# A lower least rate of filling, and outputs that begin later in their slot, in the first attention of a two-layer decoder

## The chip, the cores and the metric

The kernel runs on one core of one Trainium2 chip. The metric is the device time of the whole program in microseconds. The time before is 2068.65 us, the median of 3 runs (2068.05 to 2070.13).

## What is computed

The program is a decoder of two layers with a layer norm after each of six parts. Its input x has 8 batches of 256 tokens with 512 features, all in float32. The change touches the first part alone, a differential attention with causal mask, cut here to what matters:

```python
q = (x @ Wq.T).reshape(8, 256, 32, 16)          # 32 query heads of 16
k = (x @ Wk.T).reshape(8, 256, 8, 16)           # repeated 4 times
v = (x @ Wv.T).reshape(8, 256, 4, 32)           # repeated 8 times
scores = where(causal, einsum('bhqd,bhkd->bhqk', q, k) * 16 ** -0.5, min)
attn_out = einsum('bhqk,bhkd->bhqd', softmax(scores), v)
attn = attn_out[:, 0::2] - lambda_full * attn_out[:, 1::2]
attn = attn * rsqrt(mean(attn * attn) + eps) * ln_w * (1 - LAMBDA_INIT)
x = layernorm(x + attn.reshape(8, 256, 512) @ Wo.T)
```

After it follow a long convolution, a mixture of experts, a plain causal attention, a cross attention with a cached context and a routed attention. The second and the last attention use the same planner as the first.

## The kernel before, in words

The tokens are 16 tiles of 128. Four tiles, that is two batches, make a group, so there are four groups (0 to 3). In the first attention a *unit* is one batch and four heads: 8 units for a batch, 16 for a group, 64 in all. The function `causal_attention` (L1316) walks over *slots*, one for each unit, and some more for the tail. In slot u it does, on TensorE in this order:

- the plain scores of unit u (`maxima`, L1370). ScalarE copies them from PSUM (L1387), GpSimd masks them (L1389), and VectorE takes row maxima (L1398). The maxima of a whole batch are split into three bfloat16 terms and turned at the start of the next batch (`turn`, L1415).
- some filling work;
- the numerators of unit u - 10 (`products`, L1471), for which GpSimd has masked and added the weights;
- the weights' scores of unit u - 9 (`weights`, L1430), from which ScalarE makes the exponentials (L1458);
- the denominators of unit u - 10 (`divided`, L1491), with the reciprocal on VectorE (L1503), and then the events of the place "mid";
- filling work again, up to the scores of the next slot.

Plain scores and weights' scores share one PSUM buffer of four banks (`ps_sc`). All other results of TensorE except numerators and denominators go through three PSUM buffers (`pools`, tag "mm").

The *filling* is all other work of TensorE: turning the tiles of x of the next group, its values, keys and queries (four query blocks a batch, of four steps each), and, for each finished batch, its output. The output of a batch comes from `finish` (L510): squares on ScalarE (L580), their sums on TensorE (L532), a turn back (L545), roots on GpSimd (L561), widening on ScalarE (L557), and then for each of the two tiles a scaling (`scaled`, L568; four transposes, then a multiplication on VectorE, L577). `scaled` orders the four output steps of its tile (`out_tile`, L505), each a product of 0.86 by the planner's costs. The last step adds the residual on VectorE and starts the layer norm (`add_norm_later`, L269). In group 3 the sixteen tiles of the context are turned too, one a slot from slot 54 on (`turn_context`, L439). A tile's load into one of two buffers is issued when the tile two places before it has been turned. Tiles 8 to 15 go through one buffer (cT) from which a DMA stores them to DRAM.

The planner decides at build time which filling goes into which slot. Pieces with a due slot stand in `queue`, sorted by it; pieces without stand in `after` with the slot from which they may begin, and those come first. `fill(budget)` takes steps one after the other until at most 0.3 of its budget is left. Costs are the planner's own: 0.86 for a full product and 0.45 for four transposes. The budget of a slot is `rate` (L1610): the larger of a least rate and the sum of what is pressing (`pressure`, L1576: for each due slot, the work up to it divided by the slots that are left) and an eighth of the cost of a batch's output. The first part of it, `short` (L1613 to L1617), is filled between the plain scores and the numerators; the rest goes behind the denominators. `need(u + 1)` (L1563) does at once whatever is due in the next slot, before that slot's scores. `at(slots, place, f)` (L1526) orders an event or, with the place "fill", a piece for `after`. The engines TensorE, VectorE, ScalarE and GpSimd work in the order in which this program writes their instructions; SP issues the DMAs from its own queue.

Of the kernel before, what the change touches and what calls it, by code (L numbers as in the profile page):

```python
# [55 lines left out]
def decoder_kernel(ctx: ExitStack, tc: tile.TileContext, a: dict, out: bass.AP):  # L56
# [212 lines left out]
    def add_norm_later(work, t, ps, at):  # L269

        r = work.tile([P, D], F32, tag="row", name="res", bufs=3)
        nc.vector.tensor_tensor(r, ps, x[t], ALU.add)
        at(1, "mid", norm_later(x[t], r, lambda f: at(0, "end", f)))
# [22 lines left out]
    def diff_attention(xh, ch):  # L296
# [203 lines left out]
        def squares(n):  # L500

            n = n % 2 * KB * S
            return w[:, n : n + KB * S].rearrange("p (k s) -> p k s", k=KB)

        def out_tile(work, pools, t, yT, at):  # L505


            return out_block(pools, yT, t % 2, wo, lambda ps: add_norm_later(work, t, ps, at))

        def finish(work, pools, t0, yT, at):  # L510

            cost = 2 * (0.4 + TR + KB * MM)
            if t0 == NT - 2:
                return cost


            apart = 1 if t0 == NT - 4 else 2
            hurry = t0 == NT - 4
            wide = {}
            sq = squares(t0 // 2)  # L520

            quads = work.tile([P, 32], F32, tag="quads", name="quads", bufs=1)
            nc.vector.tensor_copy(
                quads.rearrange("p (r t) -> p r t", r=8), quad.unsqueeze(1).broadcast_to([P, 8, 4])
            )
            means = work.tile([P, S], F32, tag="means", name="means", bufs=1)

            def sums():

                ps = pools.tile([P, S], F32, tag="mm", name="ps_ss")  # L530
                for k in range(KB):
                    nc.tensor.matmul(  # L532
                        ps[32 * k : 32 * k + 32, :],
                        lhsT=quads,
                        rhs=sq[:, k, :],
                        start=True,
                        stop=True,
                    )
                nc.vector.tensor_scalar(means, ps, 1.0 / 32, EPS, ALU.mult, ALU.add)
                at(0 if hurry else 1, "end" if hurry else "mid", norms)  # L540

            def norms():
                pt = pools.tile([P, 2, P], F32, tag="mm", name="pt_ss")
                for i in range(2):
                    nc.tensor.transpose(pt[:, i, :], means[:, i * P : (i + 1) * P], ident)  # L545
                rr = work.tile([P, 2, H0], F32, tag="rrs", name="rr")
                nc.vector.tensor_copy(
                    rr.rearrange("p i (k t) -> p i k t", k=KB),
                    pt.rearrange("p i (k r t) -> p i k r t", k=KB, t=4)[:, :, :, 0],
                )  # L550
                roots(0, rr[:, 0, :])
                at(apart, "end", lambda: roots(1, rr[:, 1, :]))

            def roots(i, rr):
                def widen():
                    wide[i] = work.tile([P, H0, 32], F32, tag="wide", name="wide")
                    nc.scalar.copy(wide[i], rr.unsqueeze(2).broadcast_to([P, H0, 32]))  # L557

                def root(half):
                    r = rr[:, 8 * half : 8 * half + 8]  # L560
                    nc.gpsimd.tensor_tensor(r, r, neg_half[:, :8], ALU.pow)  # L561

                root(0)
                at(apart - 1, "end", lambda: root(1)) if apart > 1 else root(1)
                at(apart, "end", widen)
                at(apart + 1, "fill", [(TR, lambda: scaled(i))])

            def scaled(i):  # L568
                pt = pools.tile([P, KB, P], F32, tag="mm", name="pt_rr")
                for k in range(KB):  # L570
                    nc.tensor.transpose(
                        pt[:, k, :],
                        wide[i][:, 4 * k : 4 * k + 4, :].rearrange("p t d -> p (t d)"),
                        ident,
                    )
                y = yT[:, :, i * P : (i + 1) * P]
                nc.vector.tensor_tensor(y, y, pt, ALU.mult)  # L577
                at(1, "fill", out_tile(work, pools, t0 + i, yT, at))

            at(1, "start" if hurry else "end", lambda: nc.scalar.activation(sq, yT, AF.Square))  # L580
            at(1 if hurry else 2, "fill", [(0.7, sums)])
            return cost
# [733 lines left out]
    def causal_attention(name, prepare, finish, upb=KB, gather=None):  # L1316
# [18 lines left out]
        with ExitStack() as st:  # L1335
            work = st.enter_context(
                tc.tile_pool(name=f"{name}_work", bufs=2, **({"reuse_waits": "tile"} if name == "r" else {}))
            )
            ps_sc = st.enter_context(tc.tile_pool(name=f"{name}_sc", bufs=1, space=PSUM, reuse_waits="tile"))
            ps_pv = st.enter_context(tc.tile_pool(name=f"{name}_pv", bufs=1, space=PSUM, reuse_waits="tile"))  # L1340
            pools = st.enter_context(tc.tile_pool(name=f"{name}_ps", bufs=3, space=PSUM, reuse_waits="tile"))
# [23 lines left out]
            groups, negT, pT, yT = {}, {}, {}, {}  # L1365
# [160 lines left out]
            def at(slots, place, f):  # L1526


                if place == "due mid":
                    at(slots, "mid", lambda: insort(queue, f, key=lambda piece: piece[0]))  # L1530
                elif place == "fill":
                    after.append((now[0] + slots, f))
                    after.sort(key=lambda piece: piece[0])
                else:
                    events.setdefault((now[0] + slots, place), []).append(f)

            def happen(place):
                for f in events.pop((now[0], place), []):
                    f()
# [18 lines left out]
            def begin(g):  # L1558
                pieces, *groups[g] = prepare(work, pools, g, at, now[0])
                queue.extend((upg * g + slot, steps) for slot, steps in pieces)  # L1560
                queue.sort(key=lambda piece: piece[0])
# [14 lines left out]
            def pressure(u):  # L1576

                total = most = 0.0
                begun = [(due[0], current)] if current and due[0] < units + 99 else []
                for slot, steps in begun + queue:  # L1580
                    total += sum(c for c, _ in steps)
                    most = max(most, total / max(1, slot - u))
                return most

            def sums(u):
# [10 lines left out]

                return rest

            begin(0)
            need(0)  # L1600
            if name == "r":
# [2 lines left out]
            per_batch = 0.0  # L1604
            left = 0.0
            for u in range(units + lag + 2):
                now[0] = u
                happen("start")

                rate = max(2.4, pressure(u) + per_batch / upb)  # L1610
                if u < units:
                    largest = maxima(u)
                    short = max(0.0, min(0.8, rate - 1.8))  # L1613
                    if rate > 2.7:
                        short += (rate - 2.7) / 2
                    if name == "a":
                        short += MM / 2  # L1617
                    left = fill(left + short)
                    rest = sums(u)
                    if name != "a":  # L1620
                        rest()
                        happen("mid")
                    if u >= wait:
                        weights(u - wait)
                    if name == "a":
                        rest()
                        happen("mid")
                    if u % upg == upb and u // upg + 1 < NG:
                        begin(u // upg + 1)
                    left = fill(left + rate - short - MM) - need(u + 1)  # L1630

                    if u and u % upb == 0:
                        turn(u // upb - 1)
                    left = fill(left + MM)
                    largest()
                    if u % upb == upb - 1:
                        split(u // upb)
                else:

                    if u < units + wait:  # L1640
                        weights(u - wait)
                    sums(u)()
                    happen("mid")
                    left = fill(left + rate) - need(u + 1)
                    if u == units:
                        turn(B - 1)
                happen("end")
# [29 lines left out]
    def out_block(pools, yT, i, w, done):  # L1677

        return product_steps(
            lambda: pools.tile([P, D], F32, tag="mm", name="ps_o"),  # L1680
            lambda k: yT[:, k, i * P : (i + 1) * P],
            lambda k: w[:, k, :],
            done,
        )
# [758 lines left out]
```

## Time and profile before

What | Value
--- | ---
median of the runs | 2068.65 us
profiled execution, own time | 2062.48 us
its span, first to last instruction | 2060.7 us
mean granted clock of TensorE | 0.983
score copies of the first attention (L1387) | 64, from 13.88 to 378.87 us
last exponential of the first attention (L1458) | 429.88 us
last output matmuls of the first attention | 451.43 to 453.35 us
first matmuls of the convolution | 460.25 us

Between 140 and 379 us TensorE was busy 219.69 of 239 us, VectorE 189.05, GpSimd 179.11 and ScalarE 136.25. From the 10th copy (slot 9, 48.52 us) to the 64th (slot 63, 378.87 us) a slot took 6.12 us on average; the shortest took 5.22.

How to read it: a row of a timeline has the start in us, the duration, the engine, the line, the operation, what is written and read, the shape, how often, and in brackets how long the engine stood idle before and what ended that. A row of waits has who waited for whom, the sum in us, the number of times and the longest. A matmul in float32 counts as two instructions here, and neighbouring matmuls overlap, so a group's duration is a little longer than its share.

### The profile page before, as it was taken

What the parts mean: (1) busy time and instruction counts of PE and PEld (TensorE: products, weight loads), DVE (VectorE), ACT (ScalarE), POOL (GpSimd) and SP (SyncE); (2) the same over time, 40 slices, a digit from 0 to 9 for tenths busy, and PEclk for the clock granted to TensorE, in tenths of its full rate; (3) what the DMA queues carried; (4) which work ended last, traced back from release to release, by engine and by line L of the source; (5) the groups of instructions that cost most, each with busy time, mean ns of one, the idle gap of its engine ahead of it and who ended that gap; (6) DMA issues with size and microseconds to landing.
All of it is one profiled execution on the core that took longest, in us unless ns stands there. A gap on an engine that the chain in (4) does not pass through costs nothing. (4 is left out here: it accounts for less than half of the span.)

```text
span 2060.7 us, 46451 instructions
## 1 busy us (share of the span) xinstructions
PE 1921.8 (93%) x20142; PEld 1141.9 (55%) x20142; DVE 1253.7 (61%) x1933; ACT 620.1 (30%) x793; POOL 858.0 (42%) x952
## 2 busy tenths in 40 slices
PE   8979999889998998999999999998999999988885
PEld 5545555444443445666555555544888887454443
DVE  4677878758888976122234757456344544437987
ACT  4555555520010003211114434432101011245552
POOL 3687777846556823000014645333100010216763
PEclk9999999989999999999999999999999999999997
DMA  6899953315115125213232212002101000260000
GB/s 230 311 386 380 383 168 84 94 52 212 31 46 184 52 98 188 77 65 129 80 110 84 84 34 83 2 2 81 49 16 41 21 21 1 90 191 15 25 24 32
DMA packets 138044, 219.24 MB, mean 106 GB/s; under 512 B 27440, under 2 KB 52144, under 8 KB 137840
## 3 DMA queue, kind: packets, MB, share of 16 engines
q1 hardware_dynamic: 131376, 195.93, 27.9%
q0 software_dynamic: 6464, 20.32, 2.9%
q8 instruction: 161, 2.64, 0.5%
q14 instruction: 43, 0.35, 0.1%
HBM read 104.42 MB, written 123.34 MB: 111 GB/s over the span
## 5 line engine op out<-in xcount | busy, mean ns | idle before, releaser
L1503 DVE RECIPROCAL rsum<-ps_pv 128x256 f32<-128x256 f32 x128 | 224.5, 1754 | 215.6 <-PE ps_pv L1495 215.4
L182 PE MATMUL ps_y<-kv,wt 128*128 128x512 f32 x640 | 280.0, 596 | 5.2 <-POOL kv L625 2.7
L1398 DVE TENSOR_REDUCE neg<-rows 128x12 f32<-128x1536 f32 x128 | 223.0, 1742 | 53.3 <-POOL rows L1389 53.2
L1458 ACT ACTIVATE pT<-ps_k 128x1536 f32<-128x1536 f32 x128 | 185.7, 1451 | 225.4 <-PE ps_k L1450 218.4
L1459 POOL TENSOR_SCALAR_AFFINE_SELECT pT<-pT 128x1024 f32<-128x1024 f32 x128 | 141.3, 1104 | 217.4 <-ACT pT L1458 217.2
L1387 ACT COPY rows<-ps_q 128x1536 f32<-128x1536 f32 x128 | 184.2, 1439 | 151.0 <-PE ps_q L1378 96.0
L1389 POOL TENSOR_SCALAR_AFFINE_SELECT rows<-rows 128x1024 f32<-128x1024 f32 x128 | 142.3, 1112 | 183.8 <-ACT rows L1387 183.1
L182 PEld LDWEIGHTS ps_y<-kv,wt 128*128 128x128 f32 x640 | 120.8, 191 | 156.3 <-issue 137.7
L1469 POOL TENSOR_TENSOR pT<-pT 128x512 f32<-128x512 f32 x112 | 147.1, 1313 | 9.3
L212 PE MATMUL ps_f<-xT,w_l1a 128*32 128x256 f32 x2048 | 123.4, 385 | 5.5 <-ACT xT L237 4.1
L1164 PE MATMUL po_m<-dn,hT 128*128 (+1 forms) x216 | 100.8, 603 | 4.0 <-issue 2.3
L148 POOL TENSOR_SCALAR rstd<-bn_mv 128x1 f32<-128x1 f32 x80 | 15.8, 198 | 212.5 <-DVE bn_mv L156 206.4
L1143 DVE TENSOR_TENSOR h_b<-h_b,pg 128x352 f32<-128x352 f32 x36 | 18.6, 516 | 124.0 <-ACT h_b L1142 124.0
L1495 PE MATMUL ps_pv<-pT,ones_v 128*32 128x256 f32 (+1 forms) x1152 | 87.1, 381 | 5.2 <-POOL pT L1469 5.1
L212 PEld LDWEIGHTS ps_f<-xT,w_l1a 128*32 128x32 f32 x2048 | 62.9, 111 | 51.2 <-issue 9.0
L663 DVE TENSOR_REDUCE yc<-z 128x64 f32<-128x512 f32 x128 | 86.1, 673 | 5.7 <-issue 5.2
L1279 POOL DMA_INDIRECT y<-ys,slots x4 | 4.0, 1007 | 204.4 <-PE pu L182 203.8
L1378 PEld LDWEIGHTS ps_q<-kT,qT 32*128 32x128 f32 x1536 | 49.5, 188 | 50.5 <-issue 18.1
L182 PE MATMUL pg<-gu,xT_b 128*128 x216 | 72.1, 470 | 3.6 <-ACT xT_b L237 3.6
L1378 PEld LDWEIGHTS ps_q<-kz,qT 32*128 32x128 f32 x1536 | 49.2, 188 | 47.2 <-ACT pT L1458 33.7
L1378 PE MATMUL ps_q<-kz,qT 32*128 32x128 f32 x1536 | 61.5, 289 | 14.3 <-ACT pT L1458 11.6
L1378 PE MATMUL ps_q<-kT,qT 32*128 32x128 f32 x1536 | 61.9, 290 | 12.7 <-ACT pT L1458 8.7
(411 smaller groups left out, 3694.2 us busy)
## 6 DMA issues: line engine op xcount, KB each, us to landing
xs<-zero SPq DMA_DIRECT2D x8, 4352.0 KB
ys<-zero SPq DMA_DIRECT2D x8, 4352.0 KB
filters<-in_L_xattn_k SPq DMA_DIRECT2D x4, 2560.0 KB
first_h<-xs SPq DMA_DIRECT2D x36, 256.0 KB
ys<-y_m SPq DMA_DIRECT2D x36, 256.0 KB
gu<-in_L_ffn_gate_up_proj SPq DMA_DIRECT2D x3, 2816.0 KB
wt<-filters SPq DMA_DIRECT2D x32, 256.0 KB
sorted_x<-zero SPq DMA_DIRECT2D x1, 5120.0 KB
```

The costliest lines, as they stand in the source:

```text
L182: nc.tensor.matmul(ps, lhsT=lhsT(k), rhs=rhs(k), start=(k == 0), stop=(k == n - 1))
L212: nc.tensor.matmul(ps[cs], lhsT=lhsT[:, cs], rhs=rhs, start=start, stop=stop)
L1164: nc.tensor.matmul(po, lhsT=hT[:m, i, :], rhs=dn[i][:m, bass.ds(e, 1), :], start=(i == 0), stop=(i == len(FCH) - 1),)
L1378: nc.tensor.matmul(block[:, s, j, :], lhsT=q(rows, c, b * S + i * P, P), rhs=k(rows, c, b * S + keys * P, P), start=True, stop=True,)
L1387: nc.scalar.copy(d.rearrange("p j s k -> p s j k"), block)
L1389: nc.gpsimd.affine_select(out=rows, in_=rows, compare_op=ALU.is_ge, fill=-FAR, base=0, pattern=[[0, 8], [-1, P]], channel_multiplier=1,)
L1398: return lambda: nc.vector.tensor_reduce(neg[u // upb % 2][:, :, :, c], d, AX.X, ALU.max, negate=True)
L1458: nc.scalar.activation(p[:, 0:3].rearrange("p j s q -> p s j q"), block, AF.Exp)
L1459: nc.gpsimd.affine_select(out=p[:, 0:2].rearrange("p j s q -> p (j s) q"), in_=p[:, 0:2].rearrange("p j s q -> p (j s) q"), compare_op=ALU ...
L1469: nc.gpsimd.tensor_tensor(p[:, 3], p[:, 1], p[:, 2], ALU.add)
L1495: nc.tensor.matmul(ps[32 * s : 32 * s + 32, 1, j * P :], lhsT=ones_v, rhs=p[:, 1, s, :] if j else first[:, :, s, :], start=(j == 0), stop= ...
L1503: nc.vector.reciprocal(r, ps[:, 1, :])
```

## The change

Two things change in the planner's input, and no instruction is added or taken away.

First, the least rate falls from 2.4 to 1.8 for the first attention (its name is "a") and stays at 2.4 for the two others. With a rate of 1.8 the first part of the filling of a slot is 0.43 instead of 1.03.

Second, the four output steps of a tile enter the list of filling only at the place "mid" of the slot after the scaling, that is after the weights' scores and the denominators. Before, they could be the first filling of that slot, in front of numerators and weights' scores.

```diff
@@ -575,7 +575,8 @@
                     )
                 y = yT[:, :, i * P : (i + 1) * P]
                 nc.vector.tensor_tensor(y, y, pt, ALU.mult)
-                at(1, "fill", out_tile(work, pools, t0 + i, yT, at))
+                steps = out_tile(work, pools, t0 + i, yT, at)
+                at(1, "mid", lambda: at(0, "fill", steps))
 
             at(1, "start" if hurry else "end", lambda: nc.scalar.activation(sq, yT, AF.Square))
             at(1 if hurry else 2, "fill", [(0.7, sums)])
@@ -1596,6 +1597,7 @@
 
                 return rest
 
+            least = 1.8 if name == "a" else 2.4
             begin(0)
             need(0)
             if name == "r":
@@ -1607,7 +1609,7 @@
                 now[0] = u
                 happen("start")
 
-                rate = max(2.4, pressure(u) + per_batch / upb)
+                rate = max(least, pressure(u) + per_batch / upb)
                 if u < units:
                     largest = maxima(u)
                     short = max(0.0, min(0.8, rate - 1.8))
```

## The prediction

> **What bounds the kernel now.** First the page. It gives the profiled execution, 2060.7 us of span and 2062.48 us of own time, and shows TensorE as the busiest engine in every slice.
>
> ```profile
> span 2060.7 us, 46451 instructions
> ...
> PE 1921.8 (93%) x20142; PEld 1141.9 (55%) x20142; DVE 1253.7 (61%) x1933; ACT 620.1 (30%) x793; POOL 858.0 (42%) x952
> ```
>
> The change touches only the first attention, so next I read ScalarE's timeline there. Its score copies (L1387) run from 13.88 to 378.87 us, 64 of them, one for each slot; the tail of the stage ends near 457 us.
>
> ```profile
> 109.10 1.45 ACT L1458 ACTIVATE pT<-ps_k 128x1536 f32<-128x1536 f32 x1 [1.26 <-PE ps_k L1450]
> 111.62 1.44 ACT L1387 COPY rows<-ps_q 128x1536 f32<-128x1536 f32 x1 [1.07 <-PE ps_q L1378]
> 114.34 1.45 ACT L1458 ACTIVATE pT<-ps_k 128x1536 f32<-128x1536 f32 x1 [1.28 <-PE ps_k L1450]
> 116.86 1.44 ACT L1387 COPY rows<-ps_q 128x1536 f32<-128x1536 f32 x1 [1.07 <-PE ps_q L1378]
> ```
>
> That is the floor of a slot. There is one buffer for scores, so copy, weights' scores, exponential and next scores take turns: 1.44 + 1.28 + 1.45 + 1.07 = 5.24 us, of which 2.72 from copy to exponential (first half) and 2.52 from exponential to next copy (second half). Slots 18 to 23 have almost no filling and sit at this floor. Eight slots earlier it is another picture:
>
> ```profile
> 69.42 1.45 ACT L1458 ACTIVATE pT<-ps_k 128x1536 f32<-128x1536 f32 x1 [1.28 <-PE ps_k L1450]
> ...
> 72.11 1.44 ACT L1387 COPY rows<-ps_q 128x1536 f32<-128x1536 f32 x1 [0.93 <-PE ps_q L1378]
> ...
> 75.28 1.45 ACT L1458 ACTIVATE pT<-ps_k 128x1536 f32<-128x1536 f32 x1 [1.36 <-PE ps_k L1450]
> ```
>
> Here three query steps of 0.45 us stand in each half. The second half (69.42 to 72.11) took 2.69, 0.17 over; the first (72.11 to 75.28) 3.17, 0.45 over. So a first half hides 0.90 us of filling and a second half 1.18; what is beyond counts in full. Over slots 9 to 62 the excess over 5.24 is 330.35 - 54 x 5.24 = 47.4 us. This is all that the change can win in the body. The chain of waits by engine says what the excess holds besides filling:
>
> ```profile
> PE ps_o L212 <- DVE yT_b L577: 6.5, 4, 1.9
> ...
> PE ps_v L212 <- issue: 2.7, 2, 1.5
> ```
>
> Four output tiles begin in the first half of their slot, before VectorE has scaled their rows (L577), and the weights' scores queue behind them: 6.5 us, in slots 26, 40, 42 and 58. TensorE's timeline shows slot 26, 1.93 us:
>
> ```profile
> 146.05 1.92 PE L212 MATMUL ps_o<-w_l,yT_b 128*32 128x512 f32 x16 [1.93 <-DVE yT_b L577]
> 147.76 0.86 PE L1484 MATMUL ps_pv<-pT,v 128*32 128x256 f32 x16
> ```
>
> In the tail one more wait matters, with a slow TensorE behind it:
>
> ```profile
> 409.64 0.23 PE L1450 MATMUL ps_k<-negT,take 32*128 32x128 bf16 x4
> 412.10 1.51 PE L1484 MATMUL ps_pv<-pT,v 128*32 128x256 f32 x16 [2.23 <-DVE rr L471]
> 413.33 1.55 PE L1495 MATMUL ps_pv<-pT,ones_v 128*32 128x256 f32 x16
> ```
>
> The granted clock from 412 to 416 us was 0.57, and the two groups took 1.51 and 1.55 where others take 0.86 and 0.83.
>
> **The change part by part.** No instruction is added or removed. The planner's choice is arithmetic on the code's own costs (0.86 a product, 0.45 a transpose), so I followed it slot by slot, before and after. The old list agrees with the trace (the two output steps of slot 26, for one). Prices of a step from rows: output, value or key product 0.885 (16 matmuls 1.92, 24 take 2.78), query 0.45, transposed tile 0.55, scaling transposes 0.53, sums 0.45, turned maxima 0.25.
>
> *Head, slots 0 to 8* (no weights yet). Slots 3 to 6 are bound by TensorE: 0.88 of scores and 2.2 to 2.7 of filling, together 13.99 us. At a rate of 1.8 they hold 1.80, 2.25, 2.22 and 1.77, so 4 x 0.88 + 8.04 = 11.6: 2.4 less. Slots 0 to 2 win nothing (slot 2's copy waits for the lambda exponential at 22.53), nor slots 7 and 8, where turning the maxima ends a chain of copy, GpSimd, VectorE and split 6.4 us long. Head: -2.4.
>
> *Body.* The table has the excess over 5.24 in us: measured before; by the rule of 0.90 and 1.18 before; the surplus of measured over rule (waits); the rule on the new lists; what I keep of the surplus and what comes new.
>
> slots | measured | rule | surplus | new rule | new total | change
> 9-17 | 5.5 | 4.5 | 1.0 | 1.9 | 1.9 + 0.6 = 2.5 | -3.0
> 18-24 | 0.8 | 0.8 | 0 | 2.1 | 2.1 | +1.3
> 25-31 | 10.9 | 5.9 | 5.0 | 5.2 | 5.2 + 5.0 - 2.0 + 0.9 = 9.1 | -1.8
> 32-40 | 7.8 | 5.0 | 2.8 | 3.4 | 3.4 + 2.8 - 1.6 = 4.6 | -3.2
> 41-47 | 11.4 | 5.9 | 5.5 | 8.5 | 8.5 + 5.5 - 2.0 = 12.0 | +0.6
> 48-56 | 6.2 | 5.2 | 1.0 | 6.6 | 6.6 + 1.0 - 0.5 + 0.6 = 7.7 | +1.5
> 57-63 | 4.8 | 2.3 | 2.5 | 5.6 | 5.6 + 2.5 - 1.8 + 0.6 + 4.1 = 11.0 | +6.2
>
> Reading it: filling leaves slots 9 to 17 and fills the empty slots 18 to 22. The four waits on L577 go (-2.0, -1.1, -2.0, -1.8, and 0.5 each where sums and an output shared slots 35 and 51): outputs now come after the weights' scores. In slot 26 0.9 comes back, because three transposed tiles stand there in the first half and the third needs the buffer that VectorE is still reading. The price of the lower rate is late work in group 3: the planner's need for slots 41 to 46 rises to a rate of 3.65; in slots 52 and 60 a whole query block is forced in before the next scores (second halves of 3.08 and 3.97 us), and its evacuation (0.38 and the hand-overs, 0.6) then stands between it and the scores: 0.6 each.
>
> The 4.1 in the last row: the context tiles, once one a slot, pile up, and tiles 6, 7 and 8 are turned back to back in slot 62. Tile 8's load is issued only when tile 6 has been read. The nearest row is the first load of the program, 256 KB, issued at 0.80 and used at 3.59: 2.8 us. Less 0.55 for tile 7, TensorE waits 2.3 (bounds 0, if the load came sooner, and 3.1, the wait for a store at 411.27). Tile 9 follows in slot 63; its copy shares one buffer with tile 8's store and holds up the exponential by about 1.0 (0 to 3.1). A slow clock after a 2.3 us wait costs 0.8: by the 2.23 us wait above it would be 0.65 + 0.72 = 1.4, by the 1.93 us wait of slot 26, behind which the products took their normal 0.86, nothing; I take the middle.
>
> On that clock the Trainium skill has a rule ("TensorE: Matmul & The Clock Gate", Part 1, What's actually happening): the clock halves only after an idle window of about 3.4 us, which runs free. The trace disagrees, since 2.23 us was enough for a clock of 0.57. By the rule the 0.8 would be 0 and the saving in the tail below 1.4 smaller, so the sum 0.6 worse.
>
> *Tail, from 383.20 to 453.35 us.* The set of steps is the same in both lists, only their order differs. The 2.23 us wait and its slow matmuls (1.4) meet another order: -3.6. At the end, before: waits of 1.42, 0.46, 0.36 and 0.68 us; after, five output steps follow the last products and cover the 1.42, while between sums and scaling stand 2.3 us of steps against a chain of 0.17 + 1.65 + 0.40 and hand-overs, some 2.9, and the rest shrinks: -1.4. New: tiles 11 and 12 meet in slot 66 and tile 12 waits for the store of 11 (the one such wait in the trace is 3.10 us at 411.27) behind 2.2 us of other work, and two PSUM buffers come free late: +1.5. Tail: -3.5 (bounds -5.0, with no new wait, and +5, if the new waits reach TensorE twice with its slow clock).
>
> SP's queue gets the same transfers in the same order, later ones later; POOL's and VectorE's queues too. What follows the stage just starts earlier or later.
>
> Sum: -2.4 - 3.0 + 1.3 - 1.8 - 3.2 + 0.6 + 1.5 + 6.2 - 3.5 = -4.3 us. Against the profiled time 2062.48 - 4.3 = 2058.2. The median of the runs shown is 2068.65, 6.2 above that execution, so the forecast is 2064.4.
>
> **The rivals.** A difference of 0.2% is 4.1 us, about what a measurement of this kernel can tell from no change.
>
> *Full relief.* The surplus that I keep (5.0 - 2.0, 1.2, 3.5, 0.5, 0.7 and 0.6, 9.5 us in all) consists of waits of products on other engines and of two stalls marked issue. A thinner stream could dissolve two thirds of it: -6.3, so 2058. For it: slots 18 to 23 show no surplus. Against: the issue stalls (2.7 us) have nothing to do with the order of the work.
>
> *Slower: context tiles block the tail.* Tiles 11 to 15 all come later (slots 66 to 70), one buffer serves their stores, and 3.10 us on ScalarE's queue holds the exponential and, through the PSUM buffers, the products. One such wait cost 2.23 + 1.4 = 3.6 us. If none goes and two more reach TensorE, the tail is +7.2 instead of -3.5: 2064.4 + 10.7 = 2075. It decides from the second wait on. Against: between these tiles stand 3 to 5 us of matmuls.
>
> *The work only moves.* The body's sum of filling is the same; if each wait cured returns elsewhere, the time stays 2068.7.
>
> **How the numbers follow.** Forecast 0.40 (own range 2061 to 2068), full relief 0.28 (2056 to 2062), blocked tail 0.20 (2071 to 2079), only moved 0.12. Faster by more than 4.1 us: half of the forecast and all of full relief, 0.48; slower: the blocked tail and a little, 0.22; the rest 0.30. The range reaches from 2056.5 to 2073, leaving out the far half of the blocked tail and the far end of full relief.
>
> **What would show it.** Copies of slots 9 to 17 some 5.3 us apart, and the 64th copy about where it was (379 us, within 3). No wait of an output on L577 in a first half. Long slots at 44 to 46, 52 and 60, and a TensorE wait on a context load in slot 62: if that is missing, I was too dark by 3 to 4 us. The stage's last products at 450 instead of 453 us. Wrong altogether would be a second or third wait near 400 to 420 us with a clock near 0.6.

## The result: slower by 0.27%

The changed kernel takes 2070.84 us in the median against 2066.47 of the kernel before on the same chip; the ratio is 1.0027 (95% interval 1.0014 to 1.0040), that is 5.6 us slower (2.9 to 8.3); the two medians by themselves differ by 4.4 us. A second measurement on another chip, told below, gives 1.0031 (1.0018 to 1.0044). The forecast was 4.3 us faster. The time lies inside the range that was given, on the wrong side of the kernel before.

### The profile after

The profiled execution took 2070.99 us. The page says that no work was added: TensorE has its 20142 matmuls as before. The span is 8.6 us longer, and TensorE is busy for 5.7 us more with the same matmuls.

```profile
span 2069.3 us, 46444 instructions
...
PE 1927.5 (93%) x20142; PEld 1142.5 (55%) x20142; DVE 1256.2 (61%) x1933; ACT 620.3 (30%) x793; POOL 858.8 (42%) x952
```

As before the change, ScalarE's timeline gives a ruler for the first attention: the score copies (now L1388), the last exponential (L1459), and at the end of the stage the last copy into first_h. Between them the stage is 451.86 us long, where it was 443.28: 8.6 us more. The first copy comes 1.7 us later, and what follows the stage takes 1.7 us less; neither is touched by the change. In the runs below, what follows the stage takes anywhere between 1585 and 1605 us, so single spans are compared only inside the stage. The table has the lengths of its parts by the copies. The forecast's row for slots 57 to 63 held 1.0 us for slot 63, which stands with the tail here. "e15" is a second profile of the changed kernel, on another chip.

slots | before | after | e15 | change, after | forecast
--- | --- | --- | --- | --- | ---
0-8 | 34.64 | 35.60 | 35.50 | +1.0 | -2.4
9-17 | 52.64 | 51.04 | 50.95 | -1.6 | -3.0
18-24 | 37.44 | 38.96 | 38.79 | +1.5 | +1.3
25-31 | 47.61 | 48.12 | 47.60 | +0.5 | -1.8
32-40 | 54.99 | 52.27 | 52.78 | -2.7 | -3.2
41-47 | 48.09 | 49.81 | 50.61 | +1.7 | +0.6
48-56 | 53.34 | 55.79 | 55.79 | +2.5 | +1.5
57-62 | 36.24 | 40.31 | 40.25 | +4.1 | +5.2
from the 64th copy to the end of the stage | 78.29 | 79.96 | 81.93 | +1.7 | -2.5

So the losses of the forecast are there, nearly at their size: 8.6 us forecast in the four rows with a plus, 9.8 measured. The gains are not: 12.9 us forecast, and the same five rows give -1.2 in all.

TensorE's waits from 101 to 388 us show that the second part of the change did what it says. The 6.5 us of waits of outputs on the scaled rows (L577) are gone from the view; the waits for the score buffer (L1388, L1459) that stand on top are those of the floor of a slot. New are a wait for a context tile's load and one for a PSUM buffer that the layer norm's residual held.

```profile
PE ps_k L1442 <- ACT rows L1388: 7.7, 18, 0.8
PE ps_q L1379 <- ACT pT L1459: 3.0, 7, 1.1
PE pt L236 <- DMA cx<-in_ctx: 2.4, 1, 2.4
PE ps_v L212 <- issue: 2.0, 1, 2.0
...
PE pt L236 <- DVE res L272: 1.3, 1, 1.3
```

The load wait is in slot 62. In TensorE's timeline the group at 382.25 is tiles 6 and 7 behind each other (8 transposes), and tile 8, at 385.77, is not there yet. Slot 62 took 8.31 us instead of 5.24.

```profile
381.68 0.64 PE L1496 MATMUL ps_pv<-pT,ones_v 128*32 128x256 f32 x8
382.25 1.09 PE L236 MATMUL pt<-ident,cx 128*128 128x128 f32 x8
385.77 0.66 PE L236 MATMUL pt<-ident,cx 128*128 128x128 f32 x4 [2.43 <-DMA cx<-in_ctx]
386.36 0.95 PE L1379 MATMUL ps_q<-kz,qT 32*128 32x128 f32 x24
387.24 0.66 PE L236 MATMUL pt<-ident,cx 128*128 128x128 f32 x4
```

SP's queue shows why. The load at 362.92 is that of tile 7, issued when tile 5 had been turned. Those of tiles 8 and 9 are issued only at 382.94, when tiles 6 and 7 have been turned, 2.8 us before tile 8 is used.

```profile
362.92 0.34 SPq L437 DMA_DIRECT2D cx<-in_ctx  x1
363.80 0.53 SPq L446 DMA_DIRECT2D ctx_d<-first_h  x1
382.94 0.81 SPq L437 DMA_DIRECT2D cx<-in_ctx  x2
```

What stood between is slot 60, 9.51 us long where the floor is 5.24. The four output steps of a tile (two in 1.92) and a whole query block (32 matmuls, 1.91) come between 364 and 373 us; the block was due in the next slot and was put in at once, behind the last output step, and the scores wait for its evacuation (0.50).

```profile
368.75 1.92 PE L212 MATMUL ps_o<-w_l,yT_b 128*32 128x512 f32 x16
370.49 1.91 PE L212 MATMUL ps_f<-xT,w_l 128*32 128x256 f32 x32
372.90 0.95 PE L1379 MATMUL ps_q<-kz,qT 32*128 32x128 f32 x24 [0.50 <-ACT qT L1665]
```

In the tail the wait of 2.23 us at 412 us is gone, but a longer one stands near it, on a context tile whose copy to the one store buffer (cT) waits for the store of the tile before; TensorE works slowly behind it again (8 matmuls in 1.93, where 16 take 1.92). ScalarE's row comes first, TensorE's below.

```profile
414.04 0.59 ACT L237 COPY cT<-pt 128x512 f32<-128x512 f32 x1 [2.92 <-DMA ctx_d<-cT]
```

```profile
414.68 1.93 PE L212 MATMUL ps_o<-w_l,yT_b 128*32 128x512 f32 x8 [4.20 <-ACT cT L237]
```

### The profile page after: what moved, and what is told of

It is laid out like the page before. It is cut to its first block, busy times and chain, and to the rows that moved or that the text cites. A ratio compares the mean times of both kernels' runs of the same rounds, so it can differ in the third digit from the quotient of the medians.

```text
span 2069.3 us, 46444 instructions
## 1 busy us (share of the span) xinstructions
PE 1927.5 (93%) x20142; PEld 1142.5 (55%) x20142; DVE 1256.2 (61%) x1933; ACT 620.3 (30%) x793; POOL 858.8 (42%) x952
## 5 line engine op out<-in xcount | busy, mean ns | idle before, releaser
L1459 ACT ACTIVATE pT<-ps_k 128x1536 f32<-128x1536 f32 x128 | 185.8, 1452 | 211.2 <-PE ps_k L1451 195.1
L1388 ACT COPY rows<-ps_q 128x1536 f32<-128x1536 f32 x128 | 184.3, 1440 | 159.7 <-PE ps_q L1379 106.1
L1442 PE MATMUL ps_k<-qT,kz 32*128 32x256 f32 (+1 forms) x1024 | 68.8, 355 | 11.6 <-ACT rows L1388 9.7
L1442 PE MATMUL ps_k<-qT,kT 32*128 32x256 f32 (+1 forms) x1024 | 69.1, 356 | 4.7 <-ACT rows L1388 2.5
```

The source lines that it names most:

```text
L1388: nc.scalar.copy(d.rearrange("p j s k -> p s j k"), block)
L1442: nc.tensor.matmul(block[:, s, at, :], lhsT=k(rows, c, b * S + j * P, P), rhs=q(rows, c, b * S + j * P, P * (2 - j)), start=True, stop=False,)
L1459: nc.scalar.activation(p[:, 0:3].rearrange("p j s q -> p s j q"), block, AF.Exp)
```

## The experiments

Times are differences to the kernel before on the same chip, worked out as (ratio - 1) times its median there, with the interval of the ratio. Between two of the runs that stand on different chips only these differences are compared. "Stage" is the length from the first score copy to the end of the stage in the profile, less the 443.28 us of before. It comes from one execution each, and the same order of work can differ by some 2 us between two executions, as the tail of e7 shows below.

run | what | difference, us | stage, us
--- | --- | --- | ---
the change | | +5.6 (2.9 to 8.3) | +8.6
e15 | the change again | +6.4 (3.7 to 9.1) | +10.9
e1 | rate alone | +12.7 (8.8 to 16.6) | +13.7
e2 | outputs alone | -1.8 (-4.9 to 1.0) | -1.1
e3 | low rate for slots under 24 | -7.8 (-11.1 to -4.5) | -7.5
e4 | rate 2.4 in slots 0 to 8, low after | +9.0 (5.9 to 12.3) | +9.3
e6 | low rate for slots under 41 | -3.9 (-7.0 to -0.8) | -6.3
e7 | low rate under 24, outputs as before | -0.4 (-3.1 to 2.5) | -0.7
e8 | low rate from 24 on | +7.0 (4.7 to 9.0) | +8.7
e5 | the change, all context tiles in their own slots | -3.1 (-6.4 to 0.2) | +0.7
e11 | the same for tiles 0 to 8 | -1.2 (-3.7 to 1.2) | +0.4
e13 | the same for tiles 9 to 15 | +7.2 (4.5 to 9.9) | +9.1
e9 | before, all context tiles in their own slots | +2.3 (-0.4 to 5.2) | +0.6
e10 | rate alone, all tiles in their own slots | +4.3 (1.9 to 7.0) | +9.0
e12 | e3 with all tiles in their own slots | -2.7 (-6.0 to 0.8) | -2.7
e14 | e3 with all tiles due two slots later | -4.3 (-7.0 to -1.4) | 0.0

### Which part, and which slots

The change is two edits and runs through all slots, so the first four runs take it apart by edit and by slot. The theories were: the lower rate pushes work into the last group, where it is forced in and bunched (L, late work); the outputs behind the weights are the cost (O); TensorE idles in the thinly filled first slots and its clock falls (H, head).

The lower rate alone (the outputs as before):

```diff
-                steps = out_tile(work, pools, t0 + i, yT, at)
-                at(1, "mid", lambda: at(0, "fill", steps))
+                at(1, "fill", out_tile(work, pools, t0 + i, yT, at))
```

> The lower least rate alone; outputs may begin in the first half again, as before. The measured change costs 4.4 us (2066.47 to 2070.84). Theory L (late work): the lower rate is the cost, because it pushes filling of group 3 into slots 41 to 62 and bunches the context tiles. Then this kernel is slower than before by at least the same 4 us, plus what the waits of outputs on L577 cost (6.5 us before): +4 to +10 us. Theory O (outputs): beginning the outputs behind the weights' scores is the cost, the rate is a gain. Then this kernel is faster than before, -2 to -4 us.

Measured: +12.7 us. The outputs behind the weights (rate 2.4 in all slots):

```diff
-            least = 1.8 if name == "a" else 2.4
+            least = 2.4
```

> Outputs begin behind the weights' scores, the least rate stays 2.4. Theory L: the waits on L577 in slots 26, 40, 42 and 58 (6.5 us) go and little comes back, because by the rule of 0.90 and 1.18 us of hidden filling the body's excess is 29.5 instead of 29.9 us: -4 to -7 us against before, with the 64th copy about 5 us earlier against the first one. Theory O: the work that the outputs displace costs as much or more: 0 to +4 us.

Measured: -1.8 us, not to be told from nothing. Theory L had expected more: from the first to the 64th copy the profile has 365.60 us, where the kernel before has 364.99, and not 5 us less. In two of the four places the cured wait came back as others: slots 26 to 28 take 25.0 us (before 24.3), slots 42 to 44 25.6 (before 24.6). The whole change, with the low rate for the early slots alone:

```diff
-                rate = max(least, pressure(u) + per_batch / upb)
+                rate = max(least if u < 24 else 2.4, pressure(u) + per_batch / upb)
```

> The change with the lower least rate only up to slot 23, and 2.4 from slot 24 on. Theory L: the list of steps from slot 24 on is that of the outputs-only kernel, so the cost in slots 41 to 63 (about 8 us in the two profiles) is gone: faster than before by 3 to 7 us. Theory H (head): the thin filling of slots 0 to 9 leaves TensorE idle, its clock halves there and eats the gain of the early slots; then it is no better than the outputs-only kernel, and slots 0 to 23 together last as long as before (within 1 us) though less filling is in them.

Measured: -7.8 us, the fastest kernel of this study. And the whole change with the old rate in the first nine slots:

```diff
-                rate = max(least, pressure(u) + per_batch / upb)
+                rate = max(2.4 if u < wait else least, pressure(u) + per_batch / upb)
```

> The change with the least rate of 2.4 in slots 0 to 8 and 1.8 from slot 9 on. Theory H: the head is back at its length before (34.6 us from the first copy to the tenth, against 35.6 with the change) and slot 9 loses its slow matmuls, so about 2 to 3 us less than the change: +1 to +2 us against before. Theory L: slots 41 to 63 are as with the change, so it stays slower than before by 3 us or more.

Measured: +9.0 us, not better than the change; slots 0 to 8 take 35.15 us, between the change's 35.60 and the 34.64 of before. So theory O falls (the outputs alone cost nothing, and without them the low rate costs twice as much), theory H falls as the cause of the loss (the old head doesn't heal it), and the low rate behind slot 24 is the loss. What the outputs are good for shows in e1: where the rate is low and outputs may stand in front of the weights' scores, two of them still wait, one for 3.4 us, and slots 41 to 47 take 54.09 us instead of the change's 49.81. The lines are e1's waits of TensorE from 101 to 388 us.

```profile
PE ps_k L1441 <- ACT rows L1387: 7.1, 16, 0.8
PE ps_o L212 <- DVE yT_b L577: 5.5, 2, 3.4
```

### Where the late low rate costs

Three more bounds for the rate, and one combination:

```diff
-                rate = max(least, pressure(u) + per_batch / upb)
+                rate = max(least if u < 41 else 2.4, pressure(u) + per_batch / upb)
```

> The whole change, but the lower least rate ends with slot 40; from slot 41 on it is 2.4 again. Against the run that ended it at slot 24 (7.8 us faster than before) this adds the low rate of slots 24 to 40. Theory L, as it stands: the low rate costs where it pushes work into the last group, so that ending it at 41 is nearly as good as ending it at 24: 5 to 8 us faster than before, with no load wait in slot 62. Rival: any low rate behind slot 24 leaves work that is forced in later (slots 32 to 47 at their lengths of the change, 100.4 us, or longer) and the gain is half of it or less: 0 to 4 us faster than before.

Measured: -3.9 us, which lies in the rival's range, but the slots speak for theory L: stage -6.3 us, slots 32 to 47 100.42 us (e3 100.10; the change 102.08, which the expectation had added up wrongly), and slot 62 at 5.24. So the low rate of slots 24 to 40 does little harm by itself, and with the higher rate from 41 on the loss is gone. The interval doesn't separate this run from e3.

The early low rate with the outputs as before (both edits of e3 and e1 together):

> The lower least rate for the slots under 24 alone, 2.4 behind, and the outputs begin as before. With the outputs begun behind the weights the same rate was 7.8 us faster than before, and the outputs behind the weights alone were 1.8 us faster (inside the noise). If the two add up: about 6 us faster than before (4 to 8). If the gain of that run needs both (the outputs find their place only where the rate leaves room, or the other way round): within 2 us of before, or slower.

Measured: -0.4 us. By these times the gain of e3 needs both edits, though the intervals overlap with a plain sum of the two: the stage is 0.7 us shorter with the one, 1.1 with the other, and 7.5 with both. Against e7, e3 saves 2.5 us in slots 32 to 40 and 2.2 in slots 57 to 62. Why the two would not simply add up is not settled.

The complement of e3:

```diff
-                rate = max(least, pressure(u) + per_batch / upb)
+                rate = max(least if u >= 24 else 2.4, pressure(u) + per_batch / upb)
```

> The complement: the whole change, but the least rate is 2.4 for the slots under 24 and 1.8 from there on. Theory L (the late low rate is all of the loss, the early one a gain): slower than the change by what the early low rate won, about 3 to 6 us, so 8 to 12 us slower than before, with slots 57 to 61 near 32 us and slot 62 near 8.3 us as in the change. Rival (the early low rate costs by itself through TensorE's clock in the head, and the gain of the run that ended at 24 came from something else): faster than the change, 0 to 4 us slower than before.

Measured: +7.0 us, just under the range of theory L, with slots 57 to 61 at 31.99 us and slot 62 at 8.26 as expected. The early low rate wins less inside the change (1 us or so, inside the noise) than it does in e3.

### The context tiles

With the low rate, the context tiles come in bunches. To take away the bunching and leave all else, they are turned in the middle of their own slots, one a slot, outside the filling's budget:

```diff
-                    at(slot - here, "fill", [(TR, lambda i=i: turn_context(work, pools, i))])
+                    at(slot - here, "mid", lambda i=i: turn_context(work, pools, i))
```

> The whole change, but the sixteen context tiles are no longer filling work: each is turned in the middle of its own slot (54 to 69), one a slot, as it becomes due. Theory T (the bunched context tiles are the cost of the late work: tiles 7 and 8 behind each other make the load wait of 2.43 us that stretched slot 62 to 8.31 us, and tiles 9 to 15 behind each other make the wait of 4.20 us for the one buffer that the stores leave from): slot 62 comes back to 5.3 to 6 us, the wait of 4.20 us falls under 1 us, and the kernel comes 5 to 9 us under the change, to between 3 us under and 1 us over the kernel before. Theory L2 (what costs is the rest of the late work, query blocks and outputs that are forced into slots 41 to 60): the two waits go as well, but the slots 41 to 61 stay at their 137.9 us against 132.4 of before, only 1 to 3 us are won and the kernel stays 2 us or more slower than before.

Measured: -3.1 us, 8.7 under the change as its own chip had it. Slots 41 to 61 are at 136.91 us, hardly shorter than the change's 137.60, since slots 41 to 47, ahead of the edit, were 1.7 us longer in this profile. Slots 57 to 62, however, fell from 40.31 to 34.48, and the tail from 79.96 to 77.66. In TensorE's timeline of this run there is one tile in each slot, some 6 us behind the last, and no wait at any:

```profile
367.80 0.66 PE L236 MATMUL pt<-ident,cx 128*128 128x128 f32 x4
...
373.73 0.66 PE L236 MATMUL pt<-ident,cx 128*128 128x128 f32 x4
...
379.42 0.66 PE L236 MATMUL pt<-ident,cx 128*128 128x128 f32 x4
...
385.07 0.65 PE L236 MATMUL pt<-ident,cx 128*128 128x128 f32 x4
```

Of the 5.8 us of slots 57 to 62, 3.1 are slot 62 (8.31 to 5.24, the load wait) and 3.6 are slot 60 (9.51 to 5.93, the forced query block), less 0.8 elsewhere. The second is not a matter of loads. As filling, each tile takes 0.45 of a budget of about 1.8, and output steps and query block are left over for slot 60; out of the budget, they find their places in slots 54 to 61. The edit takes both away at once, and no run here tells them apart better than these two slot lengths do.

It could be that tiles in their own slots are a gain in any kernel. The same edit on the kernel before:

> The control: the kernel before, with the context tiles turned in the middle of their own slots instead of as filling work. With the whole change the same edit took 8.6 us away (from 5.6 us slower than before to 3.0 us faster). Theory T (the change bunched the context tiles, and the edit undoes the bunching): before, the tiles stood apart already (longest wait at one of them 0.3 us, slot 62 at 5.24 us), so the edit brings nothing here: within 3 us of before. Rival (turning the tiles in their own slots is a gain by itself, change or not): 5 to 9 us faster than before, and then the edit says nothing of the change.

Measured: +2.3 us, and slots 57 to 62 at 36.65 us (before: 36.24). It brings nothing where the tiles stand apart already. With the tiles out of the way in both kernels the change goes from +2.3 to -3.1 us, a gain of about 5 us where as it stands it is a loss of 5.6. That is a hint and no more: the two runs stand on different chips, and their stages (+0.6 and +0.7 us) show no gain.

On the lower rate alone (e1's edit and e5's):

> The lower least rate alone, outputs begun as before (12.7 us slower than before), with the context tiles in the middle of their own slots. Theory T: its slots 57 to 61 (32.94 us against 31.0) and its end from the last scores on (85.78 us against 78.29) are context tiles behind each other: 5 to 9 us are won, and 4 to 8 us of loss remain, which are outputs that wait for their scaled tiles (the waits of 5.5 us in two places; slots 41 to 47 at 54.09 us against 48.09). Rival (the loss is the waiting outputs alone): at most 3 us are won, 10 us or more of loss remain.

Measured: +4.3 us, 8.4 less than e1. The rest of e1's loss is the waiting outputs, as expected: its wait for L577 is as it was, and slots 41 to 47 take 54.03 us. These are its waits from 101 to 388 us.

```profile
PE ps_o L212 <- DVE yT_b L577: 5.6, 2, 3.4
```

On e3, whose tiles stand apart:

> The lower least rate for the slots under 24, the outputs behind the weights (7.8 us faster than before as it was), with the context tiles in the middle of their own slots. Theory T: the higher rate from 24 on kept the tiles apart already (slot 62 at 5.24 us, no wait over 1 us for a context tile), so nothing is left to win: within 3 us of that run, 5 to 10 us faster than before. Rival (the tiles' own slots are a gain by themselves): 11 us or more faster than before. If the tiles in the middle take the place of the filling that stood there, some of the gain can be lost as well: 3 us faster than before or less would say so.

Measured: -2.7 us, so nothing is won and perhaps some lost; 2.1 of the 4.8 us by which its stage is longer than e3's are in slots 0 to 8, which the edit doesn't touch.

Which of the waits is it? The tiles 0 to 8 alone in their own slots, in the change:

```diff
-                    at(slot - here, "fill", [(TR, lambda i=i: turn_context(work, pools, i))])
+                    if i < 9:
+                        at(slot - here, "mid", lambda i=i: turn_context(work, pools, i))
+                    else:
+                        at(slot - here, "fill", [(TR, lambda i=i: turn_context(work, pools, i))])
```

> The whole change, with the context tiles 0 to 8 in the middle of their own slots and the tiles 9 to 15 still as filling work. This splits the 8.6 us that the edit brought for all sixteen. If the load wait counts (tile 8 behind tile 7, 2.43 us at its front, slot 62 at 8.31 us, slots 57 to 61 at 32.0): slot 62 at 5.3 us, slots 57 to 61 near 29.2 us, 5 to 7 us under the change, so within 2 us of before. If the wait for the one store buffer counts (4.20 us in slot 66 and what runs slow behind it): 3 to 4 us at most are won by these tiles, the wait of about 4 us stays, and the kernel is still 2 us or more slower than before.

Measured: -1.2 us, 6.8 to 7.6 under the change, with slots 57 to 62 at 34.48 us as in e5. And yet the long wait for the store stands in its tail as before:

```profile
404.29 1.94 PE L212 MATMUL ps_o<-w_l,yT_b 128*32 128x512 f32 x8 [4.24 <-ACT cT L237]
```

The other half (`if i >= 9`):

> The whole change, with the context tiles 9 to 15 in the middle of their own slots and the tiles 0 to 8 still as filling work: the other half of the split. If the load wait in slot 62 and the slots ahead of it are nearly all of the cost (the first half won about 6.8 us): slot 62 stays near 8.3 us and slots 57 to 61 near 32.0 us, the wait for the store buffer falls from 4.2 us to under 1.5 us, and 1 to 3 us are won against the change, so 3 to 5 us slower than before. If the store wait counts as much as it is long: 4 us or more are won, within 2 us of before.

Measured: +7.2 us, where the change itself on the same chip (e15) has +6.4: nothing won. The lines behind the edit stand three further on in its rows. The store wait did go, and others took its place. In slot 62 the load wait is there; in the tail TensorE now waits 2.23 us for VectorE's means, with slow products behind it (1.36 and 1.53 us instead of 0.86 and 0.83), and the tail is 80.44 us long against 79.96 and 81.93.

```profile
384.90 0.66 PE L236 MATMUL pt<-ident,cx 128*128 128x128 f32 x4 [2.22 <-DMA cx<-in_ctx]
...
409.18 0.41 PE L548 MATMUL pt_ss<-ident,means 128*128 128x128 f32 x2 [2.23 <-DVE means L542]
```

> The change itself once more, on the chip of these runs, so that the parts are compared with it directly. As on record: 5.6 us slower than before (2.9 to 8.3), slot 62 at 8.3 us with a load wait near 2.4 us, a wait of 4.2 us for the context store behind the last scores. If slots 0 to 17, which the change was forecast to shorten by 5.4 us, come out shorter here than the 86.64 us of its first profile (the other low-rate runs lie between 82.1 and 86.5), it was one unlucky execution of them.

Measured: +6.4 us, the same waits to 0.1 us, and slots 0 to 17 at 86.45 us, as long as in the first profile. So the cost that decides the sign is in slots 57 to 62: it goes when the first nine context tiles leave the filling (with the load wait goes the forced block of slot 60, which these runs don't separate). Taking away the longest wait of the profile (4.20 us) by itself wins nothing. That the last tiles cost nothing in the tail is not shown: it is 81.34 us with the first nine tiles in their own slots, 80.44 with the last seven, and 77.66 only with all sixteen (e5), in one execution each.

### A version that beats both

e3 does, by 0.38% against before and by about 13 us against the change. A later due slot for its context tiles (slots 56 to 71):

```diff
-                    slot = 16 * g + 6 + i
+                    slot = 16 * g + 8 + i
```

> The version that was fastest (the lower least rate for the slots under 24, the outputs behind the weights), with every context tile due two slots later (62 to 77 instead of ... 54 to 69 become 56 to 71), still as filling work. Theory T: the tiles stand apart there already, so this is worth what the tail waits for the context store hold there (0.9 us): within 2 us of that version, which was 7.8 us faster than before; 5 to 10 us faster than before. Rival (its gain was the luck of one chip): within 3 us of before.

Measured: -4.3 us, just short of what theory T expected, and on another chip still faster than before by more than its noise. Slots 57 to 62 are 38.11 us (e3: 34.04), so the later slots don't help. The trace shows why: slot 59 is 10.97 us long, because TensorE waits 2.10 us in it for a tile whose load could be issued from 347 us on, when the tile two places ahead had been turned, and was issued only at 351.47, behind six issues of weights (L1961) that took SP 11.69 us; the products behind the wait take 1.51 us instead of 0.86. So a load can also come late because SP's queue is taken.

## Why the prediction was wrong

**The rule of a slot** held. Slots 11 to 14 came out at 5.26 to 5.27 us, the floor (slot 10 at 5.57). The rule of 0.90 and 1.18 us of hidden filling gave 18 to 24 (+1.3, measured +1.5) and 32 to 40 (-3.2, -2.7).

```profile
66.96 1.45 ACT L1459 ACTIVATE pT<-ps_k 128x1536 f32<-128x1536 f32 x1 [1.31 <-PE ps_k L1451]
69.48 1.44 ACT L1388 COPY rows<-ps_q 128x1536 f32<-128x1536 f32 x1 [1.07 <-PE ps_q L1379]
72.23 1.45 ACT L1459 ACTIVATE pT<-ps_k 128x1536 f32<-128x1536 f32 x1 [1.31 <-PE ps_k L1451]
74.75 1.44 ACT L1388 COPY rows<-ps_q 128x1536 f32<-128x1536 f32 x1 [0.55 <-PE ps_q L1379]
```

**The context tiles** were right in mechanism, place and nearly in size. The load wait was forecast at 2.3 us and measured 2.43; slot 60's forced block was named. The 0.8 for a slow clock behind the wait was the middle of two values, and the two profiles of the change show one each: behind 2.43 us the scores and products took their normal 0.95 and 0.86, behind e15's 2.37 us the products took 1.51. The row came out at +4.1 against 5.2. The runs put these slots at the centre: with the tiles apart they are 5.8 us shorter.

**The tail, -3.5,** is the step that failed most. Without the 1.0 of slot 63 it stood at -2.5 in the table; measured were +1.7 and, in e15, +3.6. It took the 2.23 us wait with its slow matmuls (-3.6) as gone with the order that made it, and charged the new order with 1.5. Both were off.

The old wait was worth less. In e7 the matmuls from slot 62 on come in the order of before, with the same wait, but the products behind it take their normal time (two groups of 0.86, where 1.51 and 1.55 stand before), and the tail is 76.03 us instead of 78.29:

```profile
415.82 0.86 PE L1484 MATMUL ps_pv<-pT,v 128*32 128x256 f32 x16 [2.23 <-DVE rr L471]
416.46 0.86 PE L1495 MATMUL ps_pv<-pT,ones_v 128*32 128x256 f32 x16
```

So the slow clock that the prediction read off that wait, and priced at 1.4 us, was the luck of one execution; a wait of 2.23 us doesn't always bring it. And where the old order stands with the tiles apart (e9), no wait over 0.6 us is left between 405 and 425 us, and the tail is 75.76 us. That is 2.5 less than before, slow matmuls included, and only 0.3 less than e7's (whose clock at the end of the tail was higher, 0.92 against 0.79 in e9 and 0.80 before). 3.6 us were not there to be won.

The new order cost more. A wait of 4.20 us came, with slow matmuls behind it; the four profiles that have this order (the change, e15, e4, e8) have tails of 79.25 to 81.93 us. When the wait is taken away (e13), one of 2.23 us on other data comes. I read this as a tail whose length is set by the chain of norms, roots and copies of the last batches, where one wait of TensorE more or less moves little; that reading is argued, not shown, and which part of the new order makes the tail longer stays open. The rival of the blocked tail had the place of the wait right, but its price (3.6 us a wait) is not borne out by e13.

**The head, -2.4, and slots 9 to 17, -3.0,** failed by the clock. The working asked how long TensorE works at full speed; with less filling it idles more, and is then slowed. Twelve profiles have the low rate in slots 0 to 8, four the high rate in all of slots 0 to 17 (before, e2, e8, e9). Slots 0 to 8 take 34.8 us in the mean of the twelve, against 35.4 in the five with the high rate there (e4 too): 0.6 won, not 2.4. Slots 9 to 17 take 48.97 us in five of the twelve (e1, e6, e11, e13, e14) and 50.55 to 51.04 in the other seven, the change among them, against 52.32 in the mean of the four: 3.4 or 1.4 us won, and 3.0 was forecast. The twelve have the same order of matmuls up to slot 16, so which of the two comes is the luck of an execution, and both profiles of the change had the bad case. The two windows of the change's head show the clock, 0.86 and 0.70 of full speed (the number ahead of the DMA share):

```profile
22.00:34.00 12.00, 9.36 (x160) 5.46 (x155) 6.40 (x9) 5.82 (x8) 3.07 (x3) 0.86 0.89 329
43.00:60.00 17.00, 13.67 (x180) 7.22 (x175) 7.17 (x9) 7.02 (x9) 4.91 (x5) 0.70 0.52 206
```

Before it was 1.00 and 0.90 there. From 22 to 34 us all five profiles with the high rate have 1.00, but only three of the twelve (e3, e5, e7); these three take 33.5 us for slots 0 to 8 in the mean, the nine with 0.86 take 35.2. In e13, one of the five that are quick in slots 9 to 17, the windows have 0.86 and 0.90:

```profile
43.00:60.00 17.00, 12.88 (x224) 8.17 (x224) 8.00 (x11) 9.15 (x13) 6.62 (x6) 0.90 0.52 205
```

That is a mis-sized term, not the cause of the loss: e4 has 1.00 and 0.90 as the kernel before has, and is 9.0 us slower.

**Slots 25 to 31, -1.8 (measured +0.5).** The wait on L577 in slot 26 went, and the three tiles of x that came into that first half waited for PSUM buffers, not once as I reckoned (0.9) but twice. Slot 26 is 9.02 us, where it was 8.11; slot 27 won 1.9; and slot 28 lost 1.8, with a pause of 2.02 us marked issue, which I can't explain. It is the move of the outputs that does this and not the rate: e2, with the high rate, has 9.01, 5.42 and 10.59 us there.

```profile
148.54 0.66 PE L236 MATMUL pt<-ident,x 128*128 128x128 f32 x4 [1.27 <-DVE res L272]
150.06 0.66 PE L236 MATMUL pt<-ident,x 128*128 128x128 f32 x4 [0.86 <-DVE yT_b L577]
```

**Slots 41 to 56, +2.1 (measured +4.2):** right in sign and place, too small by half.

Put together, of the 12.9 us between the forecast and the first profile's stage, the tail has 4.2 (without the 1.0 of slot 63), the head 3.4, slots 25 to 31 2.3, slots 41 to 56 2.1 and slots 9 to 17 1.4; the others cancel to within 1. (Against e7's tail, the tail's share would be 2.3 us larger.) The signs of late work came as named: slots 44 to 46 take 7.4 to 7.6 us, slot 52 7.79, slot 60 9.51, and TensorE waits for a load in slot 62. The rival "only moved" was nearer than the forecast: in slots 25 to 31, and in the tail, the waits that were cured came back as others. The blocked tail, 6.4 us slower than the median of before, was nearer still in size, but by luck: most of its loss was to be in the tail, and the tail has 1.7 to 3.6.

## What to carry to other kernels

When a rate of background work is lowered in the middle of a schedule, the work is not spared but is due at the end: look there first at whatever has a load behind it, since pieces that had a slot each now come back to back and meet the latency of their own transfer. A wait in a tail is not worth its length unless the chain behind it would really start earlier; price it by what would wait next, not by what goes. And where an engine slows after idling, thinner work ahead of a dependence chain can cost in clock a part of what it saves in work (here 5.4 us were forecast for slots 0 to 17, and 2.9 came in the mean of the twelve profiles).

## What was not expected of the hardware

The clock of TensorE was lost in whole steps. From 43 to 60 us, behind the wait of TensorE for the split maxima, the granted clock was 0.90, 0.80 or 0.70 and never between. At half speed for part of the 17 us that is 3.4, 6.8 or 10.2 us; the 0.86 in the 12 us window from 22 to 34 us is 3.4 us again. The Trainium skill ("TensorE: Matmul & The Clock Gate", Part 1, What's actually happening) says that the gate knows only full and half speed and decides over free-running windows of about 3.4 us; these steps agree with both. Idle time alone didn't tell how many such steps follow: with the high rate the wait was 3.38 us and one step followed in five of five profiles; with the low rate it was 2.73 to 2.94 us, shorter, and one step followed in five of twelve, two in one and three in six. What differs between the rates is the work around the wait, which is thinner with the low one. But the twelve have the same order of matmuls there and still differ among themselves, so the work alone doesn't fix the number; whether the rest is where the window happens to lie was not tried.
